# Logits and row maxima of the power attention in one VectorE instruction per head

## The chip, the cores and the metric

The kernel runs on one core of a Trainium2 chip. The metric is the device time of one execution in microseconds (us). Engines are named as the profile names them: PE (TensorE), DVE (VectorE), ACT (ScalarE), POOL (GpSimd), SP (SyncE, which issues most DMAs). Each engine works through its own queue in order and waits for others by semaphores.

## The reference, cut to what matters

The whole is four blocks on 16 sequences of 256 rows and 128 channels, each added to its input: a state space block, a local-attention feed-forward block, the power attention, and the feed-forward block again. Only the power attention is changed. It has 16 heads of 8 channels and degree 2:

```python
log_G = jnp.cumsum(jax.nn.log_sigmoid(gates), axis=1)      # per head, over the rows
S = Q @ K^T                                                # per head, 256 x 256
Z = 2 * jnp.log(jnp.abs(S) + 1e-7) + log(scale) + log_G[query] - log_G[key]
Z = jnp.where(causal, Z, -inf)
P = jnp.exp(Z - max(Z, axis=-1))
y = (P @ V) / sum(P, axis=-1)
```

Terms that are the same for all keys of a row (`log(scale)` and `log_G[query]`) drop out in the subtraction of the maximum. So the kernel needs, for each key, 2·log|S| plus the decay `-log_G[key]`, which is the running sum of softplus(-gate).

## The kernel before, in words

The program runs the four blocks one after the other, all on one core. In the power block the work of a sequence is cut into six pieces of 128 queries by 1024 columns. A piece of the first query half (t=0, two of them) holds 8 heads of 128 keys; a piece of the second half (t=1, four of them) holds 4 heads of 256 keys. `pieces` lists them, and 16 sequences make 96 pieces.

A piece goes through these steps, each a function of the block:

- `scores`: PE multiplies queries and keys into a PSUM tile `psc` (two buffers).
- `magnitudes`: DVE clears the sign bits of `psc` in place.
- `logarithms`: ACT takes the logarithm in place, with 1e-7 as bias.
- `logits`: DVE makes `z` in SBUF, twice `psc` plus the decays (`pdk`, or for t=0 a copy `pdk0` of the first 128 keys). This releases the buffer of `psc`.
- `maxima`: DVE reduces `z` to one maximum for each head, `mx`.
- `less_maximum`: POOL subtracts the maxima from `z`.
- `exponentials`: ACT, in place on `z`.
- `turned`: PE transposes `z` in two halves (`ppt`), ACT copies each out (`pprT`).
- `weigh`: PE multiplies by the values (`ppo`). At the end of a query half, `gather`, `turn_back` and `finish` copy, transpose and divide (`poT`, `pf`, `prl`, `py`) and add to `x_all`.

The decays of a sequence come from `gates` and `spread`. ACT makes softplus(-gate) in two parts: `pag` = log(1 + exp(-|gate|)) and `prg` = relu(-gate). `spread` adds the two on POOL, DVE scans along the rows (`png`), and SP's DMAs spread the rows of `png` over the partitions of `pdk`. POOL then masks the keys behind the query with -1e30 (`own_keys`, `causal`). Two more steps, `moments_of` and `project`, come before `gates`, and `values` after `spread`.

The order of the pieces' steps is written out by hand. One loop over `i` starts a piece every turn and lists the steps of different pieces in one turn: transposes of piece i-3, logits of i-1, magnitudes of i, maxima of i-1, scores of i+1, the logarithm of i, and so on down to the subtraction of i-1. The class `Pinned` makes each engine keep the order in which its instructions are written, so this list is the order in every queue. The steps of a later sequence's preparation (`preparing`) are put between these as the turn comes up.

All tile operations pass through `Pinned`, so in the profile they carry line 89; the tiles' names tell them apart.

## Time and profile before

| what | value |
|---|---|
| median of 9 runs | 2243.28 us (2241.48 to 2246.78) |
| the profiled execution: its own time | 2243.1 us |
| its span on the core | 2240.9 us |
| busy share of the span: PE, DVE, ACT, POOL | 91%, 84%, 77%, 85% |
| steady stretch of the power block, 1200 to 1545 us: PE, DVE, ACT, POOL busy | 287.30, 326.34, 311.18, 294.37 us of 345 |
| granted PE clock in that stretch | 1.00 |

The power block takes roughly the span from 1160 to 1560 us. Busy time is the time in which an engine has an instruction under way; it does not say which engine sets the pace. For that there are two other views: who waited for whom, and the chain of work that ended last, followed back step by step. In the lists of groups, a line gives line, engine, operation, the tiles written and read, shapes and count, then busy us, mean ns of one, and the idle time of the engine just before them with what ended it. In a timeline, a line gives start and duration in us, the engine, the operation, the tiles, and how many instructions are merged in it.

### The profile page before, as it was taken

Reading aid. Unit: us, or ns where it says so; the run is one execution under the profiler, and the core shown is the slowest. Engines: PE = TensorE matmul, PEld = TensorE weight load, DVE = VectorE, ACT = ScalarE, POOL = GpSimd, SP = SyncE. Lnnn points to the kernel's source line nnn. Section 1 sums busy time; section 2 is a strip of 40 time slices with the busy share of each in tenths; the row PEclk is TensorE's granted clock in tenths of the full one; section 3 lists DMA queues with packets and bytes.
Section 4 is the critical chain, followed back from the end, with each engine's and each line's share of the span. In section 5 each row is a group of like instructions: output and inputs, shape, how many; then the busy total and the mean of one; then the engine's idle time right before and its main releaser. Section 6 shows DMA issues by size and latency. Waiting matters only on the chain.

```text
span 2240.9 us, 43718 instructions
## 1 busy us (share of the span) xinstructions
PE 2034.0 (91%) x16172; PEld 1334.6 (60%) x16174; DVE 1892.2 (84%) x2405; ACT 1729.9 (77%) x2911; POOL 1912.4 (85%) x2199
## 2 busy tenths in 40 slices
PE   5999999878999999999967888887799999999998
PEld 2344444335677777777745666665466777777775
DVE  2999999989888888888837999998798888888883
ACT  4777777747878888787836999998688787887874
POOL 7999999959999888898847888877799998888993
PEclk8999999999999999999988999999899999999998
DMA  4333433310100000000014333331000000001110
GB/s 94 96 85 81 100 79 77 82 26 21 29 16 23 22 23 23 22 23 17 18 29 106 92 87 89 92 87 39 19 23 23 16 23 22 23 23 32 27 27 22
DMA packets 123440, 103.96 MB, mean 46 GB/s; under 512 B 53234, under 2 KB 97884, under 8 KB 123228
## 3 DMA queue, kind: packets, MB, share of 16 engines
q1 hardware_dynamic: 122540, 101.02, 19.2%
q8 instruction: 129, 2.11, 0.4%
q14 instruction: 83, 0.68, 0.1%
q10 hardware_dynamic: 688, 0.15, 0.0%
HBM read 6.78 MB, written 2.10 MB: 4 GB/s over the span
## 4 chain that ended last, share of the span: by engine, by line
PE 55%; POOL 16%; ACT 13%; issue 6%; DVE 5%; DMA 2%; SPq 1%; POOLq 0%; ACTq 0%; DVEq 0%
PE f_qk L89 8%; POOL bx L89 7%; PE f_sim L89 5%; PE f_po L89 5%; PE f_pw L89 5%; PE f_qkT_ps L89 4%; PE f_pv L89 4%; PE f_ppt L89 4%; ACT z L89 3%; PE f3m_ag L89 3%; PE f1m_ag L89 3%; ACT pprT L89 3%; ACT psc L89 3%; POOL f_m L89 3%; PE ppt L89 3%
## 5 line engine op out<-in xcount | busy, mean ns | idle before, releaser
L89 POOL TENSOR_TENSOR f_m<-f_m 128x256 f32<-128x256 f32 x512 | 360.8, 731 | 32.2 <-DVE f_m L89 31.9
L89 DVE TENSOR_TENSOR f_m<-f_qk,rope 128x1024 f32<-128x1024 f32 x256 | 308.7, 1216 | 24.7 <-POOL f_m L89 16.0
L89 DVE TENSOR_TENSOR_SCAN hs<-a,bx 128x1024 f32<-128x1024 f32 x128 | 291.3, 2281 | 38.7 <-POOL bx L89 27.2
L89 POOL TENSOR_TENSOR bx<-dx,bb 128x1024 f32<-128x1024 f32 x128 | 298.9, 2366 | 3.4 <-DVE hs L89 2.7
L89 PE MATMUL f_qk<-wqkv,f_hT 128*128 128x512 f32 x512 | 262.9, 607 | 1.8 <-ACT f_hT L89 1.8
L89 POOL TENSOR_TENSOR f_m<-f_m,f_rn 128x512 f32<-128x512 f32 x256 | 263.5, 1047 | 0.2
L89 POOL TENSOR_TENSOR f_pr<-f_pr,f_rl 128x1024 f32<-128x1024 f32 x128 | 242.0, 1902 | 24.1 <-DVE f_rl L89 16.9
L89 PE MATMUL y_ps<-hs,ident 128*128 128x512 f32 x512 | 241.2, 596 | 11.5 <-DVE hs L89 6.5
L89 ACT ACTIVATE a<-delta,neg_a 128x510 f32<-128x510 f32 x256 | 175.9, 688 | 78.8 <-DVE hs L89 73.2
L89 POOL TENSOR_TENSOR z<-z,mx 128x1024 f32<-128x1024 f32 x96 | 182.6, 1902 | 25.8 <-DVE pln_mv L103 9.6
L89 ACT ACTIVATE f_sq<-f_qk 128x512 f32<-128x512 f32 x256 | 154.6, 605 | 64.1 <-PE f_qk L89 60.0
L89 ACT COPY f_qkT<-f_qkT_ps 128x512 f32<-128x512 f32 x256 | 147.3, 590 | 62.6 <-PE f_qkT_ps L89 61.8
L89 PEld LDWEIGHTS y_ps<-hs,ident 128*128 128x128 f32 x512 | 95.1, 189 | 155.1 <-issue 126.5
L89 DVE TENSOR_REDUCE f_mx<-f_sim 128x8 f32<-128x1024 f32 x128 | 153.2, 1197 | 31.7 <-PE f_sim L89 31.7
L89 DVE TENSOR_REDUCE f_ss<-f_sq 128x8 f32<-128x512 f32 x256 | 172.8, 676 | 8.2 <-ACT f_sq L89 7.8
L89 PEld LDWEIGHTS f_qkT_ps<-ident,f_m 128*128 128x128 f32 x1024 | 120.9, 141 | 81.5 <-issue 50.9
L89 PE MATMUL ppt<-ident,z 128*128 128x128 f32 x768 | 107.5, 280 | 63.8 <-ACT z L89 43.2
L89 DVE TENSOR_TENSOR f_pr<-f_sim,f_mx 128x1024 f32<-128x1024 f32 x128 | 155.4, 1214 | 0.4
L89 DVE TENSOR_REDUCE f_rl<-f_pr 128x8 f32<-128x1024 f32 x128 | 152.7, 1193 | 1.9 <-ACT f_pr L89 1.9
L89 PE MATMUL f_sim<-f_qkT 64*64 64x128 f32 (+1 forms) x3072 | 148.3, 281 | 5.7 <-ACT f_qkT L89 4.4
L89 PE MATMUL f_qkT_ps<-ident,f_m 128*128 128x128 f32 x1024 | 146.2, 276 | 7.9 <-POOL f_m L89 7.9
L89 ACT COPY f_prT<-f_ppt 128x512 f32<-128x512 f32 x256 | 144.4, 596 | 6.5 <-PE f_ppt L89 5.8
(205 smaller groups left out, 5160.3 us busy)
## 6 DMA issues: line engine op xcount, KB each, us to landing
bb<-reps SPq DMA_DIRECT2D x128, 256.0 KB
pdk<-png SPq DMA_DIRECT2D x256, 128.0 KB
f_vx<-f_vx SPq DMA_DIRECT2D x128, 128.0 KB
f_shifted<-u_all SPq DMA_DIRECT2D x64, 64.0 KB
f_shifted<-u_all SPq DMA_DIRECT2D x64, 63.5 KB
x_all<-in_resid_dram SPq DMA_DIRECT2D x8, 256.0 KB
out_dram<-x_all SPq DMA_DIRECT2D x8, 256.0 KB
wqkv<-in_wqkv_dram SPq DMA_DIRECT2D x6, 256.0 KB
```

Of the source, the lines that this page charges most:

```text
L89: bi = getattr(self.eng, name)(*args, **kw)
```

## The change

The gate's two parts are made at half size: the factor of the relu is -0.5, and the sum of the two parts, now on DVE, halves the other part. So `png` and `pdk` hold half the decays (the mask stays at -1e30). The logits are then half size as well, log|S| plus half the decay, which is a plain addition; one instruction makes them for a head and takes that head's maximum in the same pass. The factor two is applied by the scale of the exponential. The step `maxima` is gone, and its work stands where `logits` stand.

```diff
-            act.activation(q["rg"], pg, AF.Relu, scale=-1.0)
+            act.activation(q["rg"], pg, AF.Relu, scale=-0.5)
...
-            pool.tensor_add(rg, rg, q.pop("ag"))
+            dve.scalar_tensor_tensor(rg, q.pop("ag"), 0.5, rg, ALU.mult, ALU.add)
             ng = pp.tile([P, L], F32, name=f"png_{n}", tag="ng")
             dve.tensor_tensor_scan(ng, ones, rg, 0.0, ALU.mult, ALU.add)
...
             z = pp.tile([P, nh, nk], F32, name=f"z_{n}_{t}_{c}", tag="z", bufs=5)
-            dve.scalar_tensor_tensor(
-                z.rearrange("p h k -> p (h k)"), live.pop(("ps", n, t, c)), 2.0, decay, ALU.mult, ALU.add
-            )
             mx = pp.tile([P, nh], F32, name=f"mx_{n}_{t}_{c}", tag="mx", bufs=3)
+            ps = live.pop(("ps", n, t, c))
+            for i in range(nh):
+                keys = slice(i * nk, (i + 1) * nk)
+                dve.tensor_tensor_reduce(
+                    z[:, i, :], ps[:, keys], decay[:, keys], 1.0, MASKED, ALU.add, ALU.max, mx[:, i : i + 1]
+                )
             live["z", n, t, c] = z, mx
-
-        def maxima(n, q, t, c):
-            z, mx = live["z", n, t, c]
-            dve.tensor_reduce(mx, z, AX.X, ALU.max)
...
-            act.activation(zf, zf, AF.Exp)
+            act.activation(zf, zf, AF.Exp, scale=2.0)
...
             piece(magnitudes, i)
-            piece(maxima, i - 1)
             piece(scores, i + 1)
```

## The prediction

> **What bounds the kernel now.** I read the groups of VectorE (DVE) instructions first, since the change takes work from that engine. One piece of the power attention is 1024 columns, and its three DVE passes are these rows (busy us, then mean ns of one):

> ```profile
> L89 DVE TENSOR_SCALAR psc<-psc 128x1024 int32<-128x1024 int32 x96 | 117.3, 1222 | 0.0
> L89 DVE SCALAR_TENSOR_TENSOR z<-psc,pdk 128x1024 f32<-128x1024 f32 x96 | 117.2, 1221 | 31.9 <-POOL pdk L89 11.6 <-ACT psc L89 10.0 <-issue 7.0
> L89 DVE TENSOR_REDUCE mx<-z 128x4 f32<-128x1024 f32 x64 | 77.3, 1208 | 0.0
> ...
> L89 DVE TENSOR_TENSOR py<-pf,prl 128x128 f32<-128x128 f32 x32 | 9.3, 291 | 1.2
> ...
> L89 DVE RECIPROCAL f_rl<-f_rl 128x8 f32<-128x8 f32 x128 | 26.0, 203 | 4.4
> ```

> The reader is to see that logits and maxima are about 1.2 us each, 96 times. In the windows view from 1200 to 1545 us DVE is busy 326.34 of 345 us, ACT 311.18, POOL 294.37, PE 287.30: DVE looks like the bound. The busiest engine is not always the one that sets the pace, so I asked next who waits for whom in the stage (1195 to 1555 us). For ACT the whole answer is the first line below; DVE's largest is the second:

> ```profile
> ACT pprT L89 <- PE ppt L89: 37.0, 78, 2.8
> DVE z L89 <- ACT psc L89: 10.0, 38, 0.3
> ```

> ACT never waits for DVE; DVE waits for ACT. The chain that ended last, asked between 1405 and 1430 us, agrees: it has no DVE entry. One turn of it:

> ```profile
> 1420.14 0.92 ACT psc L89
> 1421.05 0.98 ACT z L89
> 1422.03 0.04 issue
> 1422.07 0.67 PE ppt L89 x4
> ...
> 1422.83 0.40 ACT pprT L89
> ...
> 1423.31 0.59 ACT pprT L89
> 1423.90 0.92 ACT psc L89
> ```

> Logarithm, exponential, transposes on PE, copies, next logarithm: ACT with one hop over PE. The pace is the distance between logarithms on ACT. The timeline of ACT over one sequence (six pieces):

> ```profile
> 1427.54 1.03 ACT L89 ACTIVATE psc<-psc 128x1024 f32<-128x1024 f32 x1
> ...
> 1431.30 1.03 ACT L89 ACTIVATE psc<-psc 128x1024 f32<-128x1024 f32 x1
> ...
> 1435.30 1.03 ACT L89 ACTIVATE psc<-psc 128x1024 f32<-128x1024 f32 x1
> ...
> 1440.30 1.02 ACT L89 ACTIVATE psc<-psc 128x1024 f32<-128x1024 f32 x1
> ...
> 1444.00 1.02 ACT L89 ACTIVATE psc<-psc 128x1024 f32<-128x1024 f32 x1
> ...
> 1447.75 1.03 ACT L89 ACTIVATE psc<-psc 128x1024 f32<-128x1024 f32 x1
> ```

> With the next at 1451.51 the distances are 3.76, 4.00, 5.00, 3.70, 3.75, 3.76: 23.97 us for a sequence, 16 sequences. By the magnitudes on DVE just before, the first of these logarithms is of the second first-half piece (t=0, eight heads of 128 keys); the next four are t=1 pieces (four heads of 256), the last is the first t=0 piece of the next sequence. The 5.00 and 4.00 hold the gates and an extra copy of the preparation.

> **The change part by part.** *What DVE gives up.* In order, one instruction starts before the former ends:

> ```profile
> 1411.85 0.23 DVE L103 BATCH_NORM_AGGREGATE pln_mv<-pln_st 128x2 f32<-128x6 f32 x2
> ...
> 1441.35 1.23 DVE L89 SCALAR_TENSOR_TENSOR z<-psc,pdk 128x1024 f32<-128x1024 f32 x1 [0.35 <-ACT psc L89]
> 1442.49 1.22 DVE L89 TENSOR_SCALAR psc<-psc 128x1024 int32<-128x1024 int32 x1
> 1443.62 1.21 DVE L89 TENSOR_REDUCE mx<-z 128x4 f32<-128x1024 f32 x1
> ```

> Start to start is 1.13 us: 1024 columns at 1.04 ns (the slope between the 1024 and the 128 column rows, 930 ns over 896) are 1.066, and 0.064 is fixed. Logits and maxima cost 2.26 us of DVE a piece.

> *What it gets.* The built program shows that "one instruction per head" is two: the fused one, and one that writes a 128x1 column of maxima. So 17 or 9 DVE instructions a piece instead of 3. Main instruction, start to start: 128 x 1.04 + 64 ns = 0.197 us (py at 1424.84 is followed by z at 1425.05: 0.21), and 256 x 1.04 + 64 ns = 0.330. For the small one the first line above is nearest: two in 0.23 us at 160 ns each, so 0.07 apart. Pairs are 0.267 and 0.400: X = 8 x 0.267 = 2.13 us for t=0, 4 x 0.400 = 1.60 us for t=1. The running maximum costs no second cycle in TENSOR_REDUCE (1208 ns), so I take one cycle per column; TENSOR_TENSOR_SCAN takes two (2281 ns for 1024) and is the other end. DVE's work for the two steps falls from 2.26 to 1.60 or 2.13. That alone would move nothing, for DVE is not on the chain.

> *What moves, the decisive part.* DVE's order is written out. Before: logits i-1, magnitudes i, maxima i-1. Now the maxima are inside the logits, ahead of magnitudes i. The next logarithm on ACT needs magnitudes i, and the logits need the last logarithm. So there is a loop: logarithm (1.03), hop to DVE (0.03 to 0.10 above, taken 0.07), X, magnitudes (1.22), hop to ACT (0.03: ended 1189.96, ACT started 1189.99 at the stage's start). That is 2.35 + X. Before, X was 1.13 and the loop 3.48, hidden below every distance. Now it is 4.48 for t=0 and 3.95 for t=1. Each distance becomes the larger of the old one and the loop of its piece, as ACT is serial and keeps no slack between pieces: 4.48, 4.00, 5.00, 3.95, 3.95, 4.48 = 25.86. That is +1.89 a sequence, x16 = +30 us.

> *Bounds of the pair.* Near end, the column for nothing: X 1.57 and 1.32, distances 3.92, 4.00, 5.00, 3.70, 3.75, 3.92, +0.32 x 16 = +5. Middle, the column waits until the main instruction has ended (291 and 421 ns, then 70): X 2.89 and 1.96, 28.41 a sequence, +71. Far end, each followed by a full RECIPROCAL-like 203 ns: X 3.95 and 2.50, 32.15, +131. Two cycles a column: X 3.20 and 2.67, 31.18, +115. I take +30, since every pair of independent DVE instructions in the timeline overlaps by 0.08 or so.

> [...]

> *Who waits behind.* The scores of piece i+1 wait for the logits to free their bank (two buffers), with weigh, turn-back and the next transposes behind them on PE. That round spans two pieces: 1.03 + 0.07 + 2.13 + 1.16 (scores) + 0.64 (weigh) + 1.09 (transposes) + 1.07 (copies) = 7.2, below two distances (over 7.9): hidden. POOL's subtraction gets its maxima earlier (X after the logits start instead of 3.47); ACT's exponential never waited for it: nothing.

> *The rest.* The sum of the gates' halves goes from POOL (726 ns x 16 = 11.6 us) to DVE before the scan: 0.33 us at one cycle, 0.63 at two (the scan's own distance). It stands with scan (0.63), reciprocal and py (0.49) behind the magnitudes of the piece after the gates, 1.5 to 1.8 us, under a logarithm that starts late because of the 5.00 distance; uncovered it would be 16 x 0.33 to 0.63 = 5 to 10 us. The other DVE fill also falls under a logarithm, where the maxima stood. Scale factors on ACT: Abs 0.39 and scaled Relu 0.40 us on the same tile, so nothing, at most 96 x 0.01 = 1 us. The order on PE, ACT and SP is unchanged, DMAs too. At the start of the stage the first logits last 1 us longer and the shorter gate step gives 0.4 back: left out.

> Sum: the profiled execution took 2243.1 us (span 2240.9), the median is 2243.28; 2243.1 + 30 = 2273.

> **The rivals.** *Pairs do not overlap* (for: the second instruction hands out a result of the first; against: all neighbours in the timeline overlap): +71, 2314; to +131 at the far end. *ACT's chain stays the bound, not slower.* For: it is the chain now, and DVE has less to do. Its point: 2.35 + X under 3.76 and 3.70, so pairs under 0.176 and 0.338. The first is below a lone 128 column instruction's 0.197, so fixed costs would have to shrink as well. It gives 2243, or 2242 with the start shorter; a real gain would need ACT or its hop over PE to get shorter, which no edit touches. *Half gain:* the column nearly free, 2248.

> **How the numbers follow.** Forecast case 0.54 (2260 to 2285); pairs not overlapped or two cycles 0.26, of which 0.22 lies up to 2325; column nearly free 0.09 (2248 to 2260); chain unchanged 0.11. The range is 2247 to 2325; it leaves out the unchanged case and 0.04 above, 0.15 in all. Measurement tells 0.2% (4.5 us) from no change: the unchanged case splits into same 0.06 and faster 0.05 for what I have not seen; 0.02 of the nearly free case counts as same; slower is the rest, 0.87.

> **What would show it.** In the profile after: the column instruction near 0.07 us from its neighbour; ACT's psc with idle time released by DVE psc (none in the stage now), about 0.7 us on t=0 pieces; logarithms 4.5 and 3.95 apart; DVE's entries in the chain; DVE's busy share lower in the stage though the stage is longer. I am wrong if ACT still waits only for PE, or if pairs stand 0.36 us or more apart at 128 columns.

## The result and the profile after

The changed kernel took 2271.7 us (median of 10 runs, 2267.03 to 2281.82), the kernel before 2244.14 us on the same chip: a ratio of 1.0124 with a 95% interval of 1.0114 to 1.0134, slower by 28 us. The forecast was 2273 (2247 to 2325). The profiled execution took 2268.23 us with a span of 2266.5 us, 25.6 us more than the span before. The number was right; of the sum behind it, one term was three times too large and two terms were missing.

The groups of DVE instructions, forms apart (busy us, mean ns of one, then idle time and its releasers), show what the two rows of 1.22 us a piece have become:

```profile
L89 DVE CUSTOM_DVE_ANT_0 z<-psc,pdk 128x256 f32<-128x256 f32 x256 | 93.3, 421 | 82.8 <-ACT psc L89 47.8 <-POOL z L89 24.0 <-issue 9.8
L89 DVE CUSTOM_DVE_ANT_0 z<-psc,pdk 128x128 f32<-128x128 f32 x256 | 56.7, 286 | 31.9 <-ACT psc L89 17.1 <-POOL pdk L89 12.4 <-POOL pln_r L107 1.2
L89 DVE DVE_READ_ACCUMULATOR2_ANT mx<- 128x1 f32 x512 | 42.6, 83 | 0.0
```

As foreseen there are two instructions for a head. What a pair costs is read from the starts in DVE's timeline (start, duration), here of a t=0 piece:

```profile
1446.47 0.29 DVE L89 CUSTOM_DVE_ANT_0 z<-psc,pdk 128x128 f32<-128x128 f32 x1 [2.31 <-ACT psc L89]
1446.69 0.08 DVE L89 DVE_READ_ACCUMULATOR2_ANT mx<- 128x1 f32 x1
1446.69 0.29 DVE L89 CUSTOM_DVE_ANT_0 z<-psc,pdk 128x128 f32<-128x128 f32 x1
...
1447.95 0.29 DVE L89 CUSTOM_DVE_ANT_0 z<-psc,pdk 128x128 f32<-128x128 f32 x1
1448.16 0.08 DVE L89 DVE_READ_ACCUMULATOR2_ANT mx<- 128x1 f32 x1
1448.16 1.23 DVE L89 TENSOR_SCALAR psc<-psc 128x1024 int32<-128x1024 int32 x1
```

The column read has its 0.08 us, but the next head's main instruction starts at the same moment. Eight pairs take 1448.16 − 1446.47 = 1.69 us, 0.211 each, against the prediction's 0.267. At 256 columns pairs stand 0.345 apart (0.400 predicted), as in the same timeline:

```profile
1426.50 0.42 DVE L89 CUSTOM_DVE_ANT_0 z<-psc,pdk 128x256 f32<-128x256 f32 x1 [1.07 <-ACT psc L89]
...
1426.85 0.42 DVE L89 CUSTOM_DVE_ANT_0 z<-psc,pdk 128x256 f32<-128x256 f32 x1
```

So X is 1.69 and 1.38 us, not 2.13 and 1.60, and 2.35 + X is 4.04 and 3.73.

The waits in the stage (1195 to 1580 us; total us, times, longest), the first two of ACT's, then two of DVE's:

```profile
ACT pprT L89 <- PE ppt L89: 43.5, 80, 2.5
ACT psc L89 <- DVE psc L89: 11.9, 30, 1.3
```

```profile
DVE z L89 <- ACT psc L89: 63.8, 55, 3.3
...
DVE pln_mv L103 <- POOL pln_mr L109: 8.8, 9, 1.4
```

ACT's wait for DVE's `psc` is new: it is the loop, in some turns made longer by the last line's wait. That one is new too, and nothing in the prediction stands for it. The chain that ended last can be followed back only to 1575 us, into the last sequence; there it holds DVE's pairs and magnitudes of one t=0 turn:

```profile
1575.39 0.20 DVE z L89
1575.60 0.20 DVE z L89
1575.81 1.15 DVE psc L89
...
1576.99 1.01 ACT psc L89
```

The timeline of ACT over one quiet sequence, logarithms only:

```profile
1469.89 1.01 ACT L89 ACTIVATE psc<-psc 128x1024 f32<-128x1024 f32 x1
1474.00 1.01 ACT L89 ACTIVATE psc<-psc 128x1024 f32<-128x1024 f32 x1 [0.26 <-DVE psc L89]
1478.10 1.01 ACT L89 ACTIVATE psc<-psc 128x1024 f32<-128x1024 f32 x1 [0.26 <-DVE psc L89]
1481.89 1.01 ACT L89 ACTIVATE psc<-psc 128x1024 f32<-128x1024 f32 x1
1486.86 1.02 ACT L89 ACTIVATE psc<-psc 128x1024 f32<-128x1024 f32 x1
...
1494.46 1.01 ACT L89 ACTIVATE psc<-psc 128x1024 f32<-128x1024 f32 x1
```

From here on pieces are numbered 0 to 5 in a sequence (0 and 1 are t=0), and a "distance" is the time from a piece's logarithm to the next piece's. Before they were 3.76, 3.76, 4.00, 5.00, 3.70, 3.75 = 23.97 us. Now they are 4.11, 4.10, 3.79, 4.97, and the last two together 7.60: 24.57. The loop costs 0.60 us a sequence, a third of the 1.89 predicted.

But only few sequences are so quiet. Most are longer at two other places. The windows view, three windows of 3.41 us around one turn of the gates (length, then busy us and instructions of PE, PEld, DVE, ACT, POOL, then the granted clock and DMA):

```profile
1300.77:1304.18 3.41, 3.41 (x37) 2.32 (x36) 2.17 (x8) 3.08 (x6) 2.49 (x2) 1.00 0.31 71
1304.18:1307.59 3.41, 1.86 (x14) 1.44 (x16) 3.34 (x11) 3.12 (x9) 0.00 (x0) 1.00 0.02 5
1307.59:1311.00 3.41, 3.41 (x29) 2.35 (x26) 2.54 (x10) 2.51 (x4) 3.09 (x3) 0.50 0.27 65
```

PE is busy 1.86 of 3.41 us while ACT makes the gates, and in the next window it runs at half clock. In the steady stretch (1205 to 1560 us) the record holds nine such stretches, each a multiple of 3.41 us, 44 us in all; the kernel before holds none between 1195 and 1574. Most of them, six of the nine, follow the gates' turn of a steady sequence: the distance after piece 4 goes from 3.8 to 4.77, and to 5.9 where the stretch is twice as long.

Adding up the distances of the profiled execution, from the first logarithm of the stage to the last (417.6 us, before 388.0):

| what | us |
|---|---|
| the loop: 13 steady sequences x 0.60 | 7.8 |
| distances lengthened by half clock in these | 12.5 |
| moments waiting for POOL ahead of piece 1's logits, less what later distances give back | 3 |
| the first sequence: 1.8 at its first distance, 1.9 with a half-clock stretch of 3.4 us behind its gates | 3.7 |
| the last two sequences | 2.5 |
| sum | 29.5 |

Outside this stretch the profiled execution is 4.0 us shorter, which makes the 25.6 us of the span.

### The profile page after: what moved, and what is told of

It is laid out like the page before. It is cut to its first block, busy times and chain, and to the rows that moved or that the text cites. A ratio compares the mean times of both kernels' runs of the same rounds, so it can differ in the third digit from the quotient of the medians.

```text
span 2266.5 us, 44541 instructions
## 1 busy us (share of the span) xinstructions
PE 2054.0 (91%) x16172; PEld 1346.1 (59%) x16174; DVE 1828.1 (81%) x3253; ACT 1735.2 (77%) x2911; POOL 1901.3 (84%) x2183
## 5 line engine op out<-in xcount | busy, mean ns | idle before, releaser
L89 POOL TENSOR_TENSOR f_m<-f_m 128x256 f32<-128x256 f32 x512 | 360.7, 730 | 32.2 <-DVE f_m L89 32.0
L89 DVE TENSOR_TENSOR f_m<-f_qk,rope 128x1024 f32<-128x1024 f32 x256 | 308.7, 1216 | 24.6 <-POOL f_m L89 16.1
L89 DVE TENSOR_TENSOR_SCAN hs<-a,bx 128x1024 f32<-128x1024 f32 x128 | 291.3, 2281 | 39.1 <-POOL bx L89 27.6
L89 POOL TENSOR_TENSOR bx<-dx,bb 128x1024 f32<-128x1024 f32 x128 | 298.9, 2365 | 3.5 <-DVE hs L89 2.7
L89 PE MATMUL f_qk<-wqkv,f_hT 128*128 128x512 f32 x512 | 263.4, 607 | 1.8 <-ACT f_hT L89 1.8
L89 POOL TENSOR_TENSOR f_m<-f_m,f_rn 128x512 f32<-128x512 f32 x256 | 263.4, 1046 | 0.2
L89 POOL TENSOR_TENSOR f_pr<-f_pr,f_rl 128x1024 f32<-128x1024 f32 x128 | 241.9, 1901 | 24.2 <-DVE f_rl L89 17.0
L89 PE MATMUL y_ps<-hs,ident 128*128 128x512 f32 x512 | 241.2, 596 | 11.5 <-DVE hs L89 6.5
L89 DVE CUSTOM_DVE_ANT_0 z<-psc,pdk 128x256 f32<-128x256 f32 (+1 forms) x512 | 150.0, 354 | 114.7 <-ACT psc L89 64.8
L89 ACT ACTIVATE a<-delta,neg_a 128x510 f32<-128x510 f32 x256 | 175.9, 688 | 78.7 <-DVE hs L89 73.1
L89 ACT ACTIVATE f_sq<-f_qk 128x512 f32<-128x512 f32 x256 | 154.5, 605 | 62.5 <-PE f_qk L89 58.5
L89 POOL TENSOR_TENSOR z<-z,mx 128x1024 f32<-128x1024 f32 x96 | 182.1, 1897 | 23.8 <-DVE mx L89 17.0
L89 ACT COPY f_qkT<-f_qkT_ps 128x512 f32<-128x512 f32 x256 | 147.3, 590 | 63.6 <-PE f_qkT_ps L89 62.8
L89 PEld LDWEIGHTS y_ps<-hs,ident 128*128 128x128 f32 x512 | 95.1, 189 | 155.2 <-issue 126.5
L89 DVE TENSOR_REDUCE f_ss<-f_sq 128x8 f32<-128x512 f32 x256 | 172.8, 676 | 8.2 <-ACT f_sq L89 7.8
L89 DVE TENSOR_REDUCE f_mx<-f_sim 128x8 f32<-128x1024 f32 x128 | 153.2, 1197 | 31.7 <-PE f_sim L89 31.7
L89 PE MATMUL ppt<-ident,z 128*128 128x128 f32 x768 | 113.7, 291 | 67.4 <-ACT z L89 47.1
L89 PEld LDWEIGHTS f_qkT_ps<-ident,f_m 128*128 128x128 f32 x1024 | 121.1, 142 | 82.5 <-issue 50.6
L89 DVE TENSOR_TENSOR f_pr<-f_sim,f_mx 128x1024 f32<-128x1024 f32 x128 | 155.4, 1214 | 0.4
L89 PE MATMUL f_qkT_ps<-ident,f_m 128*128 128x128 f32 x1024 | 146.7, 276 | 8.5 <-POOL f_m L89 8.5
L89 DVE TENSOR_REDUCE f_rl<-f_pr 128x8 f32<-128x1024 f32 x128 | 152.7, 1193 | 1.9 <-ACT f_pr L89 1.9
L89 PE MATMUL f_sim<-f_qkT 64*64 64x128 f32 (+1 forms) x3072 | 147.1, 280 | 4.2 <-ACT f_qkT L89 2.9
```

The costliest lines, as they stand in the source:

```text
L89: bi = getattr(self.eng, name)(*args, **kw)
```

## The experiments

Each ratio is against runs of the kernel before on the same chip.

**1. Is it the place of the logits? Magnitudes first.** The changed kernel, with two lines exchanged:

```diff
-            piece(logits, i - 1)
             piece(magnitudes, i)
+            piece(logits, i - 1)
```

> The changed kernel, but in each turn DVE issues the magnitudes of piece i ahead of the logits of piece i-1. Theory A (the order closes a loop logarithm, logits with maxima, magnitudes, next logarithm, of 2.35 us plus the logits): the loop now spans two pieces (about 4.0 us against 7.5), ACT's chain sets the pace again at 23.97 us a sequence, and the time is 2239 to 2247 us; the granted PE clock of the stage is back at 1.00. Theory B (the many short DVE instructions cost the time, wherever they stand): it stays between 2262 and 2275 us.

Measured: 2283.72 us, ratio 1.0184 (1.0165 to 1.0202), slower still, and outside both ranges. The loop is gone: the distances after pieces 0 and 1 are 3.75 again in most sequences. But the one after piece 2 is mostly 4.98 to 5.14 instead of 4.00. The waits of this kernel (DVE's, then PE's) name the reason:

```profile
DVE psc L89 <- PE psc L89: 104.6, 79, 3.3
```

```profile
PE psc L89 <- DVE mx L89: 28.2, 40, 2.0
```

The scores need the bank that the logits free, the logits now stand behind the magnitudes, and the next magnitudes need the scores. The prediction held this round to be hidden; it is, as long as the logits come first. Some 60 us of half clock in the steady stage come on top. The loop was a cost, but taking it away in this manner opens a dearer one.

**2. Is there a loop at all? The kernel before, with its maxima put ahead of the magnitudes**, which makes X 2.26 us without any new instruction:

```diff
             piece(logits, i - 1)
+            piece(maxima, i - 1)
             piece(magnitudes, i)
-            piece(maxima, i - 1)
```

> The kernel before, with its long instructions, but with the maxima of piece i-1 moved ahead of the magnitudes of piece i. Theory A: the loop is 2.35 + 2.26 = 4.61 us, which stands above all distances between logarithms but the one of 5.00, so 28.05 us a sequence, 65 us more in 16: 2308 us, and up to 25 us more where the PE clock drops to half as PE waits. Theory B: no new instruction is in it, 2243 us.

Measured: 2341.18 us, ratio 1.0429 (1.0411 to 1.0446). This is 8 us above the expected 2308 and its 25 us for the clock. The distances are 4.69 to 4.77 at most pieces, apart from the gates' turn and half clock; by the prediction's sum they are 2.35 + 2.26 = 4.61. ACT waits for DVE, as in ACT's timeline of this kernel (logarithms only):

```profile
1419.90 1.02 ACT L89 ACTIVATE psc<-psc 128x1024 f32<-128x1024 f32 x1
1424.67 1.01 ACT L89 ACTIVATE psc<-psc 128x1024 f32<-128x1024 f32 x1 [0.92 <-DVE psc L89]
1429.44 1.01 ACT L89 ACTIVATE psc<-psc 128x1024 f32<-128x1024 f32 x1 [0.92 <-DVE psc L89]
```

The loop is confirmed, and its size to within 0.16 us. The time above the loop's price goes with 22 half-clock stretches, 167 us in all.

**3. Is it PE's clock? More work for PE.** The changed kernel, with the products of `weigh` issued a second time in half of the turns, the gates' among them (they write the same values again; `weigh` takes a flag for it):

```diff
...
+            if i % NPC in (0, 1, 3):
+                for b in range(2):
+                    piece(weigh, i - 3, b, True)
```

> The changed kernel; in three of six turns, where PE then waits about 1 us for the exponential, its 16 products with the values (0.58 us) are issued a second time, onto the same result. Theory C (of the 28 us, about 10 are the loop with pairs of 0.21 and 0.345 us, and the greater part of the rest are stretches at half PE clock that follow windows with PE busy 0.54 to 0.6): the stage's granted clock is 1.00, a sequence takes 24.6 to 25 us, and the time is 2252 to 2260 us. Theory D (the half clock is only a by-product of waiting and costs nothing by itself): 2268 to 2278 us, as PE has only more to do.

Measured: 2260.78 us, ratio 1.0075 (1.0063 to 1.0087), 11 us less than the changed kernel though PE does more. One half-clock stretch of 3.4 us is left in the steady stage. That is 0.8 us above the first theory's range and 7 us below the second's. What stays is the loop and the distance after piece 1, 4.95 in many sequences.

**4. The other half of the change alone.** The kernel before with decays made at half size, the sum of the gate's parts on DVE and the scale 2 in the exponential, but logits and maxima as they were:

```diff
-            act.activation(q["rg"], pg, AF.Relu, scale=-1.0)
+            act.activation(q["rg"], pg, AF.Relu, scale=-0.5)
...
-            pool.tensor_add(rg, rg, q.pop("ag"))
+            dve.scalar_tensor_tensor(rg, q.pop("ag"), 0.5, rg, ALU.mult, ALU.add)
...
-                z.rearrange("p h k -> p (h k)"), live.pop(("ps", n, t, c)), 2.0, decay, ALU.mult, ALU.add
+                z.rearrange("p h k -> p (h k)"), live.pop(("ps", n, t, c)), 1.0, decay, ALU.mult, ALU.add
...
-            act.activation(zf, zf, AF.Exp)
+            act.activation(zf, zf, AF.Exp, scale=2.0)
```

> The kernel before with one part of the change alone: decays at half size with the sum of the gate's parts on DVE, and the factor two in the exponential; logits and maxima stay two long instructions in their old places. Both theories: this part lies under other work, 2241 to 2246 us. If the move of the sum from POOL to DVE mattered, it would show as 5 to 10 us.

Measured: 2262.19 us (2250.47 to 2271.42), ratio 1.0085 (1.0058 to 1.0112). Missed by 16 us. Nearly all distances are those of the kernel before; the exceptions are those after the gates' turn, where half-clock stretches (51 us in the steady stage) make 4.77 or 5.9 of 3.70. An edit that by itself lengthens next to nothing (0.06 to 0.12 us after piece 0 in some sequences) costs 18 us, and the half clock is what its profile shows for it.

**5 and 6. More work for PE in kernel 4, and in the kernel before as a control.** The diff is that of experiment 3.

> The kernel before with the half-size decays alone (which took 18 us more at the same distances between logarithms, with 51 us of the steady stage at half PE clock), and with the products with the values issued twice in the three turns where PE waits. Theory E (its loss is the PE clock alone, and that drops after a stretch of about 3.4 us in which both waits of the gates' turn fall): no half clock in the steady stage, 2242 to 2248 us. Rival (the sum on DVE or the scales cost the time): 2256 to 2266 us.

> The control: the kernel before with the same products issued twice in the same three turns. Its profile has no half clock in the steady stage, and the doubled products lie in waits of PE, so 2241 to 2246 us by every theory. Were it faster than before by over 5 us, other executions of before would have half-clock stretches that its profile does not show; slower by over 5, the doubled products cost by themselves.

Measured: 2254.5 us, ratio 1.0040 (1.0024 to 1.0055), and for the control 2252.12, ratio 1.0032 (1.0021 to 1.0042). The first gains 8 us over experiment 4 with only two stretches of 3.4 us left. The control shows that the second products cost 8 us by themselves (the distance after piece 1 is 4.45 to 4.80 instead of 3.75 in nine sequences). Both expectations had put that at nothing, and both were missed by 6 to 7 us. So experiment 3 shows less than the whole of what the clock takes: 11 us, and perhaps up to 8 more.

**7. Is it the kernel, or where its waits fall? The kernel before, begun later.** One memset of 1638 columns on DVE, ahead of the first scan of the block and nowhere else:

```diff
+        late = w.tile([P, 1638], F32, name="late")
...
+            if n == 0:
+                dve.memset(late, 0.0)
             dve.tensor_tensor_scan(ng, ones, rg, 0.0, ALU.mult, ALU.add)
```

> The kernel before with nothing changed but a start of the power block's steady stage later by 1.7 us: a memset of 1638 columns on DVE ahead of the first scan. Theory E in its stronger form (before keeps full clock only because its 23.97 us period is close to seven windows of 3.41 us and its waits happen to straddle a window's edge): half-clock stretches appear in the stage at distances otherwise unchanged, 2250 to 2268 us. Rival (before is immune, the drops come from longer waits in the other kernels): 2244 to 2247 us, full clock.

Measured: 2254.0 us (2239.06 to 2271.12), ratio 1.0035 (1.0009 to 1.0061). In the profiled execution the distances are those of the kernel before, except after the gates' turn. ACT's timeline, a sequence's first logarithm and the last three up to the next sequence's first, with 4.77 where the kernel before has 3.70:

```profile
1285.13 1.03 ACT L89 ACTIVATE psc<-psc 128x1024 f32<-128x1024 f32 x1
...
1301.64 1.02 ACT L89 ACTIVATE psc<-psc 128x1024 f32<-128x1024 f32 x1
1306.41 1.02 ACT L89 ACTIVATE psc<-psc 128x1024 f32<-128x1024 f32 x1
1310.16 1.03 ACT L89 ACTIVATE psc<-psc 128x1024 f32<-128x1024 f32 x1
```

The windows view of the same place:

```profile
1298.55:1301.96 3.41, 2.12 (x16) 1.52 (x16) 3.41 (x5) 3.12 (x9) 2.06 (x3) 1.00 0.02 5
1301.96:1305.37 3.41, 3.41 (x30) 2.74 (x27) 3.06 (x5) 2.17 (x4) 2.91 (x3) 0.50 0.32 66
```

Eight stretches, 48 us. The runs' times follow the mean granted clock: 2239.06 us at 0.982, 2271.12 at 0.961. The written order is unchanged; what differs is where the gates' turn falls between the windows. In the traces of the kernel before and of the changed one all changes of the granted clock, from the first to the last, lie on one grid of 3.413 us to within 0.004 us (651 and 659 steps), and a window is a step of it. The traces show the position: the time from a window's edge to the logarithm of piece 3, behind which ACT makes the gates. In the sequence shown it starts at 1296.64, 1.51 us behind the edge at 1295.13. Of the 13 steady sequences of this run, the eight at 1.42 to 2.82 us have a drop behind the gates, the five at 1.07 to 1.35 have none; in the kernel before all 13 lie at 0.44 to 1.29, and none has one. In the changed kernel the six at 1.59 to 2.62 have one, the seven at 0.23 to 1.20 and at 2.97 have none. (Experiment 10 has two at 2.68 and 2.82 without one.) The period of the kernel before, 23.97 us, is near seven windows of 3.413 us (23.89), so that a position moves by only 0.08 us from one sequence to the next, and a good or a bad one lasts for many. Why nearly all executions of the kernel before find a good position is not shown by one trace of each: of the 99 that were timed beside the changed kernel and the experiments, 94 took 2238 to 2249 us, the other five 2254 to 2266 at mean clocks of 0.964 to 0.970.

**8. Moments in the written order.** Experiment 3 with the moments issued through DVE's written order, behind the magnitudes of a sequence's first piece:

```diff
-    def moments(pool, src, n, name):
+    def moments(pool, src, n, name, dve=nc.vector):
...
-            nc.vector.bn_stats(st[:, i, :], src[:, i, :])
-            nc.vector.bn_aggr(mv[:, i, :], st[:, i, :])
+            dve.bn_stats(st[:, i, :], src[:, i, :])
+            dve.bn_aggr(mv[:, i, :], st[:, i, :])
...
-            q["found"] = moments(pp, x_all[:, 2 * n : 2 * n + 2, :], 2, f"pln_{n}")
+            q["found"] = moments(pp, x_all[:, 2 * n : 2 * n + 2, :], 2, f"pln_{n}", dve)
```

> The changed kernel with the products issued twice (2260.8 us, with the logarithms after the second t=0 piece up to 4.97 us apart instead of 4.11), and with the layer norm's moments of the power block kept on DVE where they are written, behind the magnitudes of a sequence's first piece. Theory F (there the moments stood ahead of the second piece's logits and waited up to 1.4 us for POOL's factors of an earlier sequence): no such wait, all sequences near 24.57 us, 2252 to 2257 us. Rival (the long distance has another cause): 2259 to 2263 us.

Measured: 2262.39 us, ratio 1.0072 (1.0056 to 1.0087), missed, and inside the rival's range. The distance after piece 1 is 4.11, as expected, in nearly every sequence; the one after piece 0 has become 4.64. So the moments and their wait had made the distance after piece 1 long, and the move has lengthened another.

**9. Three moves that use DVE's new room.** On the changed kernel: the copy `pqk` from ACT to DVE, the moments in DVE's written order one turn earlier, and magnitudes ahead of logits in one turn of six.

```diff
-            act.copy(q["qk"], q.pop("pqk"))
+            dve.tensor_copy(q["qk"], q.pop("pqk"))
...
-        LEAD = 12
-        preparing = (moments_of, turn, project, gates, spread, values)
+        LEAD = 13
+        preparing = (moments_of, hold, turn, project, gates, spread, values)
...
+            if i % NPC == 1:
+                piece(magnitudes, i)
+                piece(logits, i - 1)
+            else:
+                piece(logits, i - 1)
+                piece(magnitudes, i)
```

`hold` only yields twice; the moments take `dve` as in experiment 8.

> The changed kernel with three edits that use the room the change made on DVE. (a) The copy of the queries and keys (pqk, 512 columns) goes from ACT to DVE, so the gates' turn on ACT loses about 0.46 us start to start. (b) The moments of the next sequence go through DVE's written order, one turn earlier, behind the magnitudes of a sequence's last piece. (c) Where the second piece of a sequence starts, its magnitudes stand ahead of the first piece's logits, in that one turn only. Theory G (what is left of the loss is the loop at t=0, the moments' wait behind POOL and the half clock of PE after the gates' turn): the distances between logarithms after pieces 0 to 5 become 3.76, 4.11, 3.78, 4.5, 3.81, 3.79 = 23.75 us instead of 24.57 to 26; against the 23.97 of the kernel before that is -3.5 us over 16 sequences, and up to 20 us of half clock may stand on top: 2239 to 2258 us, under the changed kernel in any case. Rival H (the order by hand already holds the best of it, and moved work only opens another wait, as in the two earlier edits of the order): one of the distances grows to 4.5 or more and the time stays at 2262 to 2285.

Measured: 2288.74 us, ratio 1.0195 (1.0181 to 1.0208), missed. The copy did more than hoped: the distance after piece 3 is 4.12, not 4.97. The moments did harm. ACT's timeline:

```profile
1463.58 0.88 ACT L89 ACTIVATE pxn<-x_all,pln_mr,pln_r 128x128 f32<-128x128 f32 x2 [1.57 <-POOL pln_mr L110]
```

ACT waits 1.57 us for POOL's part of the moments, the distance after piece 0 grows to 5.26, and 89 us of half clock fall on the stage. In the last two sequences, which prepare nothing, the distance after piece 0 is 3.73: the exchange in one turn works.

**10. The changed kernel, begun later** by the memset of experiment 7.

> The changed kernel, with only the memset of 1638 columns on DVE ahead of the first scan that moved the kernel before by +10 us on the median. Theory E (the kernel before keeps full clock because its period of 23.97 us nearly equals seven windows of 3.41 us, so that a lucky position lasts; the changed kernel's period of 24.6 us or more slides through all positions, so its loss to the half clock is a mean and does not hang on where the stage begins): the median stays within 8 us of the changed kernel's, 2264 to 2280, and the profile shows again some 40 to 60 us of half clock in the steady stage, in other sequences. Rival I (the changed kernel too has a position of its own that was unlucky): the time moves by more than 10 us, to under 2260 or over 2285.

Measured: 2272.66 us (2269.02 to 2290.55), ratio 1.0147 (1.0122 to 1.0172), 1 us from the changed kernel by the median, 5 us by the ratio, and with an interval that meets its. The profiled run is the slowest of its six, with 99 us of half clock in the stage, more than the 40 to 60 expected; the median is as expected. A change of the start that costs the kernel before 10 us costs the changed one nothing that can be told.

**11 and 12. The two moves that worked, and a cure for the moments.** The diff of experiment 11 against the changed kernel; experiment 12 adds the exchange in one turn of six from experiment 9.

```diff
...
-            q["found"] = moments(pp, x_all[:, 2 * n : 2 * n + 2, :], 2, f"pln_{n}")
+            q["found"] = moments(pp, x_all[:, 2 * n : 2 * n + 2, :], 2, f"pln_{n}", bufs=B)
...
-            act.copy(q["qk"], q.pop("pqk"))
+            dve.tensor_copy(q["qk"], q.pop("pqk"))
```

> The changed kernel with two edits only: the copy of the queries and keys (pqk) goes from ACT to DVE, as in the run before, where the gates' turn was 4.12 us long by it instead of 4.97; and the moments' tiles get one buffer for each of the 16 sequences instead of two, so that no moments have to wait for POOL to read the ones of two sequences before (32 pairs of small instructions then stand at the start of the stage, where DVE is idle for most of 1154 to 1163 us). Theory G (loop at t=0, moments' wait, half clock after the gates' turn make up the loss): distances after pieces 0 to 5 of 4.11, 4.11, 3.78, 4.12, 3.81, 3.79 = 23.72 us in every sequence, against 23.97 before, thus -4 us, and with the gates' turn short little half clock is left in the steady stage: 2236 to 2250 us. Rival H (an edit of the order only opens another wait): one distance at 4.5 or more, half clock as in the changed kernel, 2262 to 2285.

> As the kernel with the copy on DVE and a buffer for each sequence's moments, and in the one turn where the second piece of a sequence starts its magnitudes stand ahead of the first piece's logits. Theory G: the loop at t=0 is left in one turn of a sequence instead of two; distances 3.75, 4.11, 3.78, 4.12, 3.81, 3.79 = 23.36 us, -0.6 us a sequence against before and -10 us in all; with little half clock 2230 to 2246 us, under the kernel before. Rival H: scores on PE wait for the logits that now come later, the distance after piece 0 or 1 grows over 4.5, and the time is that of the kernel without the swap or up to 20 us more.

Measured: 2248.56 us (2245.15 to 2254.17), ratio 1.0024 (1.0011 to 1.0037), and 2241.04 us (2237.31 to 2244.43), ratio 0.9984 (0.9966 to 1.0002). All of DVE's waits in experiment 11's stage:

```profile
DVE z L89 <- ACT psc L89: 35.7, 33, 2.6
DVE z L89 <- POOL pdk L89: 14.3, 12, 1.5
DVE z L89 <- POOL pln_r L106: 10.7, 9, 1.2
DVE z L89 <- POOL z L89: 9.0, 10, 1.4
DVE z L89 <- issue: 4.8, 9, 0.6
```

The moments' wait is gone, most sequences are 23.73 us, and no half clock stands between 1216.6 and 1537.4 us. (The third line stands ahead of piece 1's logits, which start 0.14 us after the logarithm has ended; the distance there is 4.11.) What is left stands at the ends: the first logarithm comes 3.8 us later than before, the first sequence takes 4.0 us longer, with 6.8 us of half clock behind its gates, and the last two 2.4 us. With the exchange the distance after piece 0 is that of the loopless kernel; ACT's timeline, logarithms only:

```profile
1376.25 1.01 ACT L89 ACTIVATE psc<-psc 128x1024 f32<-128x1024 f32 x1
1379.97 1.03 ACT L89 ACTIVATE psc<-psc 128x1024 f32<-128x1024 f32 x1
1384.10 1.01 ACT L89 ACTIVATE psc<-psc 128x1024 f32<-128x1024 f32 x1 [0.26 <-DVE psc L89]
...
1399.61 1.01 ACT L89 ACTIVATE psc<-psc 128x1024 f32<-128x1024 f32 x1
```

23.36 us a sequence, 0.6 less than before. In its profiled execution the 13 steady sequences take 6.3 us less than before, and they begin 3.7 us later. The median is 2.2 us under that of the kernel before, which is within 0.2% and cannot be told from no change; against the changed kernel it is some 31 us.

## Why the prediction was right, and where it was not

*The mechanism was right.* Logits that hold the maxima stand ahead of magnitudes, and a loop of logarithm, logits and magnitudes overtakes ACT's chain. Experiment 2 makes the loop larger and the distances follow; experiments 1 and 12 take it away and 3.75 is back.

*The pair was mis-sized.* The step "For the small one the first line above is nearest: two in 0.23 us at 160 ns each, so 0.07 apart" failed: a pair takes 0.211 us. Less the 0.197 worked out for a lone main instruction that leaves 0.014 us for the column, and less the 0.21 between the starts of a lone 128 column row and its neighbour in the kernel before next to nothing:

```profile
1424.84 0.29 DVE L89 TENSOR_TENSOR py<-pf,prl 128x128 f32<-128x128 f32 x1
1425.05 1.21 DVE L89 SCALAR_TENSOR_TENSOR z<-psc,pdk 128x1024 f32<-128x1024 f32 x1
```

With the right X the prediction's own sum gives, after pieces 0 to 5, 4.04, 4.04, 4.00, 5.00, 3.73, 3.75 = 24.56. The measured period is 24.57, though single distances differ by up to 0.2 (4.11 and 3.79 where the sum has 4.04 and 4.00). So the loop alone is worth 13 to 16 times 0.60, 8 to 10 us, which makes a time near 2252: the place of the rival "half gain", not of the forecast case. Each main instruction starts 0.08 us before the former one ends (0.29 long and 0.211 apart at 128 columns, 0.42 and 0.345 at 256), much as the neighbours in the prediction's rows do, so the pairs are not the dearer ones of the rival. There are two instructions for a head, as the built program had it: 512 rows of the column read and 256 + 256 of the main one.

*The clock was missing.* The prediction has no term for PE's clock: it was 1.00 in the stage before, and the sum leaves it there. It turned out to change with where the waits fall: 12.5 us of the profiled execution's loss, and experiments 3, 4, 7 and 11 move it in both directions: of the changed kernel's 44 us at half clock 3.4 are left in 3 and none between 1216.6 and 1537.4 us in 11, and the kernel before, with none in its stage, has 51 us with 4's edit and 48 with 7's. With a period of 24.6 us, 0.7 beyond seven windows, and more where a wait lengthens it, the changed kernel's gates wander from 0.23 to 2.97 us behind a window's edge, and its drops behind the gates stand where they are at 1.59 to 2.62. Experiment 10 is in line with that; no run varied the period alone.

*The moments were missing.* "The other DVE fill also falls under a logarithm, where the maxima stood" failed. The moments (lines 102 to 110) do not pass through `Pinned`, other than was said of all tile operations above, so the written order does not hold them. With two buffers they must wait until POOL has read the moments of two sequences before. In the kernel before, DVE has no such wait in the stage; now it stands between magnitudes and the logits of the loop. Row from the changed kernel's DVE timeline:

```profile
1295.17 0.25 DVE L103 BATCH_NORM_AGGREGATE pln_mv<-pln_st 128x2 f32<-128x6 f32 x2 [1.38 <-POOL pln_mr L109]
```

Experiment 11's buffers take it away, and the distance after piece 1 is 4.11 in nearly all sequences.

*What held.* DVE's busy share fell (216.35 of 300 us from 1250 to 1550, before 283.82 from 1200 to 1500), and the time rose. The scores' round and the gates' sum on DVE cost no distance in quiet sequences.

So the result fell near the forecast by luck: two errors met. In the profiled execution the loop took about 9 us (7.8, and 1.4 in the last two sequences) where 30 were put, 21 too much; the other 16 of its 25.6 us (clock, moments, start, less what is saved elsewhere) had no term. A sum that hits is not yet a sum that is right; only the rows of after tell.

## What to carry to other kernels

An instruction that does two steps in one moves the second step to the place of the first; ask which loop that place lies on before counting what the engine saves. Where PE has short idle turns, do not carry the granted clock of the profile of before over to the changed order (here it was 1.00 in the stage, and the changed order had 44 us at half clock there): look for the stretch in which PE is least busy, and for slack in that turn. Room that a change makes on one engine is worth something only when work from the bounding engine is moved into it, as the copy here, which took 0.85 us off the longest distance.
